# Empty instructions on TensorE from a fixed list, and the statistics' loads at other places, in a two-layer image block

## The chip, the core and the metric

The kernel runs on one core of a Trainium2 chip. The time is device microseconds of one execution. The engines are called PE (TensorE, the products; PEld is its loading of weights), DVE (VectorE), ACT (ScalarE), POOL (GpSimd) and SP (SyncE, which here only starts transfers).

## What is computed

Eight images of 384 channels and 64x64 pixels, in fp32, go through two layers, each with a residual. In the reference, with a group norm of 32 groups ahead of each layer:

```
# layer 0: layer norm over channels, qkv; the first 192 channels attend in 8x8 windows,
# the other 192 in windows shifted by 4 (4 heads of 48 each, bias by relative position)
x = x + proj(concat(win_attn(w1), win_attn(shifted w2, mask)))
# layer 1
t = einsum('bchw,oc->bohw', gn(x), w_in)            # 1x1 convolution
t = irfft2(rfft2(8x8 patches of t) * fft_filter)
t = depthwise_conv3x3(t, w_dw)
x = x + einsum('bchw,oc->bohw', gelu(t[:, :192]) * t[:, 192:], w_out)
```

## The kernel before

An image is cut into 8 strips of 8 rows (512 tokens, 3 channel tiles of 128 partitions). A *unit* is one strip of one of the two attention branches, so an image has 16 units; even units begin a strip. Everything of unit u is written as pieces with a place on a line, `at(place, piece, ...)` (L299), for example the three `qk_tile` pieces of a unit at 0.14, 0.34 and 0.55 of the unit before (L454; 3 channel tiles of weights, so 3 products of 512 columns each, written to pq), then `v_tile` (pvv), `scores` (pS, 64 small products), `exponent` and `divide` on DVE and ACT (tile e), `turn` (pT, transposes of e), `apply` (pA, 64 small products) and `put`; `project` (pr) is the output projection with its residual, three pieces a strip. Layer 1 of image b lies two units behind its own layer 0 and so beside layer 0 of image b+1: `mix` (pt, the 1x1 convolution), `transform` (pf, the 8x8 patches forward, then a product with feff on DVE), `back` (pz, inverse), `conv` (the 9 taps of the depthwise filter on DVE, tile zz, L758), `gate`, and `finish` (pw, the output product and residual x_finish). The plan is sorted by place at the end (L908), and that order is the program order of PE. All products are fp32 and take two passes, so a `matmul` gives four PE instructions (two weight loads, two products), a transpose two.

The helper `matmul` (L60) issues one product and then up to `share` empty instructions (`nop`, hint "empty") from the number that its piece has been given. The number comes from the end of the function (L908 to L926): at each marker `small_tiles` (L331, which itself does nothing) it takes the count of PE instructions so far, estimated from the table `FETCHES` and a guess of the waits, and finds n, the empties that bring the marker's run of small tiles to a given place modulo 256 (`RUN_AT`). If n is under 132, it spreads n over the `qk_tile` and `project` pieces since the last `scores`; otherwise it gives none. A marker stands ahead of two kinds of run: at the end of even units for images 1 to 7 (ahead of `ln_sums`, `transform`, `apply`, `transform`, `scores`: ln 32, pf 32, pA 128, pf 32, pS 128, 352 PE instructions, a *mixed run*), and at the end of odd units (ahead of `back`: pz 192, pA 128, pS 128).

Loads go through SP's queue; a load that is marked so waits for the first qk tile of its unit (`in_dense_work`, L325). A strip's *statistics* (L344: BNStats on DVE, tile st, fed by x_stats, 768 KB) feed the group norm of the first layer. For image b over 0 they are taken during image b-1, one strip per odd place and half a unit apart from its load (L806 to L812); `input_mean` and `input_std` follow in unit 10. The other loads of 768 KB a strip are x_norm, x_add, x_mix and x_finish, and out is stored.

Of the kernel before, what the change touches and what calls it, by code (L numbers as in the profile page):

```python
# [25 lines left out]
C_ID, C_ONES, C_GRP, C_FWD, C_INV, C_MASK = 0, 128, 256, 384, 512, 640  # L26
C_PICK = C_MASK + 3 * 64
N_CONST = C_PICK + 2
WAITS = 6.42, -38
FETCHES = {"qk_tile": 12, "v_tile": 24, "project": 12, "scores": 128, "apply": 128, "turn": 16,  # L30
           "ln_sums": 32, "mix": 12, "transform": 32, "back": 192, "finish": 48, "input_mean": 4,
           "input_std": 4, "second_mean": 4, "second_std": 4, "filter_weights": 4, "out_bias": 36,
           "qk_weights": 48, "spread_first": 16, "v_weights": 60}
RUN_AT = 208, 138


@with_exitstack
def block_kernel(ctx: ExitStack, tc: tile.TileContext, out, x, consts, fsel, wqk, wv, bqk, bv,
# [16 lines left out]

    fetched = {"count": 0, "empty": 0, "share": 0}

    def matmul(*args, **kw):  # L60
        tc.keep_in_program_order(nc.tensor.matmul(*args, **kw))  # L61
        fetched["count"] += 4

        n = min(fetched["empty"], fetched["share"])
        for _ in range(n):
            tc.keep_in_program_order(nc.tensor.nop(hint="empty"))
        fetched["empty"] -= n
        fetched["count"] += n

    def transpose(*args, **kw):  # L70
        tc.keep_in_program_order(nc.tensor.transpose(*args, **kw))  # L71
        fetched["count"] += 2

    def strip(tag, bufs, name):
        return sb.tile([P, KC, ST], F32, tag=tag, bufs=bufs, name=name)
# [85 lines left out]
    def filter_weights():  # L161
        pf = psum("pf")
        matmul(pf[:, 0:C], fsel_sb, filt_sb, start=True, stop=True)
        for h in range(2):
            nc.vector.tensor_copy(feff[h * 64:(h + 1) * 64], pf[h * 64:(h + 1) * 64, h * 192:(h + 1) * 192])
# [45 lines left out]
    def centre(w, *key):  # L211
        for k in range(KC):
            nc.scalar.activation(w[:, k], w[:, k], AF.Copy, scale=lng_sb[:, k:k + 1])
        pc = psum("pc")
        for k in range(KC):
            matmul(pc[:, 0:C], ones_c, w[:, k], start=(k == 0), stop=(k == KC - 1))
        means[key] = w, pc
# [5 lines left out]
    def qk_weights(br):  # L223
        pb = all_biases()[:, 3 * br:3 * br + 3]
        for j in range(3):
            for k in range(KC):
                matmul(pb[:, j:j + 1], wqk_sb[:, k, 3 * br + j, :], lnb_sb[:, k:k + 1],
                       start=(k == 0), stop=(k == KC - 1))
        centre(wqk_sb[:, :, 3 * br:3 * br + 3].rearrange("p k j c -> p k (j c)"), "qk", br)
# [71 lines left out]
    def at(place, piece, *args):  # L301
        plan.append((place, len(plan), piece, args))
# [64 lines left out]
    def summed(b, s):  # L367

        return b > 0 or s > 2
# [179 lines left out]
    def turn(b, s, br):  # L549

        nm = f"{b}_{s}_{br}"
        e = qks.pop((b, s, br, "e"))
        pT = psum2(f"pT_{nm}")
        for i in range(NS):
            transpose(pT[:, i // 4, i % 4 * P:(i % 4 + 1) * P], e[:, 2 * i:2 * i + 2, :], ident)
        eT = sb.tile([P, 2, ST], F32, tag="eT", bufs=1, name=f"eT_{nm}")
        nc.scalar.copy(eT, pT)
        qks[b, s, br, "eT"] = eT
# [163 lines left out]
    on_pe = {(B - 1, s): {1: 5} for s in range(NS - 1)}  # L722
# [83 lines left out]
    for b in range(B):  # L806
        first = 2 * NS * b

        for s in range(NS):
            u = first - 14.84 + s if b else -10 + 0.1 * s  # L810
            at(u, load, b, s, "stats")
            at(u + (0.5 if b else 0.05), input_stats, b, s)  # L812
        if b == 0:
# [18 lines left out]
        for s in range(NS):  # L832
            u = first + 2 * s
# [46 lines left out]
        for s in range(NS):  # L880
            u = first + 2 + 2 * s
# [24 lines left out]


    order = [p[2:] for p in sorted(plan, key=lambda p: p[:2])]  # L908
    count, dense, empty = fetched["count"], [], [0] * len(order)
    for i, (piece, args) in enumerate(order):  # L910
        count += 4 * sum(on_pe[args].values()) if piece is conv_taps else FETCHES.get(piece.__name__, 0)
        if piece in (qk_tile, project):
            dense.append(i)
        elif piece is scores:
            dense = []
        elif piece is ln_sums and not summed(*args):
            count += 64
        elif piece is small_tiles:
            n = (RUN_AT[args[0] % 2] - count - round(WAITS[0] * args[0] + WAITS[1])) % 256
            if n < 132:  # L920
                count += n
                for j in range(n):
                    empty[dense[j % len(dense)]] += 1
    for (piece, args), n in zip(order, empty):
        fetched["empty"], fetched["share"] = n, (n + 2) // 3
        piece(*args)  # L926
    assert fetched["count"] == count

# [103 lines left out]
```

## Time and profile before

| what | value |
|---|---|
| times of three runs, us | 3568.28, 3572.18, 3581.91 |
| median, us | 3572.18 |
| span of the profiled execution, us | 3571.7 |
| instructions in it (all engines) | 93732 |
| mean DMA rate, GB/s | 120 |
| DVE, depthwise taps L758 (zz), x1483 | 1117.8 us busy |
| PE, qk products (pq), x2160 | 999.8 us busy |
| PE, mix products (pt), x1536 | 536.0 us busy |
| PE, projection products (pr), x1152 | 522.5 us busy |
| SP's x_stats loads, x56, 768 KB each | 7.6 us from issue to landing |
| DVE wait for x_stats, 10 times | 19.1 us |

The profiled execution gives no time of its own apart from its span; the span lies 0.5 us below the median, and is what a sum from rows is made against. The second part of the page shows the span in 40 slices: the clock that TensorE was granted is full in all but the first slice, and PE is busy at nine tenths or more from the second slice to the last but one. A product's time in the rows is modelled at its end, so the distance between the starts of two of them is the better figure: six pq products take 2.57 us.

A row "issue" in the chain of waits is time in which an engine waited for nothing that the profile shows. Empty instructions have no rows of their own in the groups; they are counted in the built program, as is the place of an instruction modulo 256.

### The profile page before, as it was taken

Reading aid. Unit: us, or ns where it says so; the run is one execution under the profiler, and the core shown is the slowest. Engines: PE = TensorE matmul, PEld = TensorE weight load, DVE = VectorE, ACT = ScalarE, POOL = GpSimd, SP = SyncE. Lnnn points to the kernel's source line nnn. Section 1 sums busy time; section 2 is a strip of 40 time slices with the busy share of each in tenths; the row PEclk is TensorE's granted clock in tenths of the full one; section 3 lists DMA queues with packets and bytes.
Section 4 is the critical chain, followed back from the end, with each engine's and each line's share of the span. In section 5 each row is a group of like instructions: output and inputs, shape, how many; then the busy total and the mean of one; then the engine's idle time right before and its main releaser. Section 6 shows DMA issues by size and latency. Waiting matters only on the chain.

```text
span 3571.7 us, 93732 instructions
## 1 busy us (share of the span) xinstructions
PE 3489.3 (98%) x36598; PEld 2209.2 (62%) x36598; DVE 3059.8 (86%) x4370; ACT 2475.3 (69%) x3983; POOL 953.0 (27%) x1616
## 2 busy tenths in 40 slices
PE   7999999999999999999999999999999999999998
PEld 5666666666666666666666666666666656666554
DVE  4766689889988899888998889988899888887988
ACT  4777677768777677776777767777777768776442
POOL 5333222223222232222232223222232223221000
PEclk8999999999999999999999999999999999999999
DMA  4333333234333334333333334333334233333431
GB/s 124 115 124 111 104 113 133 101 105 158 127 121 116 114 125 158 103 112 134 126 130 124 118 106 143 133 103 134 123 120 148 100 106 122 100 104 108 156 116 72
DMA packets 177254, 427.45 MB, mean 120 GB/s; under 512 B 26784, under 2 KB 29371, under 8 KB 176840
## 3 DMA queue, kind: packets, MB, share of 16 engines
q1 hardware_dynamic: 139984, 370.54, 29.6%
q0 software_dynamic: 36416, 50.65, 5.1%
q8 instruction: 318, 5.21, 0.6%
q14 instruction: 96, 0.79, 0.1%
q10 hardware_dynamic: 440, 0.27, 0.0%
HBM read 270.21 MB, written 100.79 MB: 104 GB/s over the span
## 4 chain that ended last, share of the span: by engine, by line
PE 88%; DVE 8%; ACT 2%; DMA 1%; issue 1%; SPq 0%; ACTq 0%; DVEq 0%
PE pq L61 26%; PE pr L61 14%; PE pvv L61 13%; PE pt L61 11%; PE pw L61 6%; DVE zz L758 4%; PE pA L61 4%; PE pz L61 3%; PE pS L61 3%; PE pT L71 3%; PE pf L61 2%; PE ln L61 1%; DVE t L679 0%; DMA x_stats<-in_x_dram 0%; DVE e L535 0%
## 5 line engine op out<-in xcount | busy, mean ns | idle before, releaser
L758 DVE SCALAR_TENSOR_TENSOR zz<-z,dw_sb,zz 128x512 f32<-128x512 f32 x1483 | 1117.8, 783 | 26.2 <-ACT z L716 14.9
L61 PE MATMUL pq<-y,wqk_sb 128*128 128x512 f32 x2160 | 999.8, 600 | 0.9 <-DVE y L436 0.8
L613 POOL DMA_DIRECT2D oT<-o x960 | 480.4, 508 | 981.3 <-ACT z L716 442.4
L61 PEld LDWEIGHTS pq<-y,wqk_sb 128*128 128x128 f32 x2160 | 400.7, 190 | 459.9 <-issue 416.1
L61 PE MATMUL pt<-wi_sb,xn 128*128 128x384 f32 x1536 | 536.0, 487 | 7.6 <-ACT kcd L468 4.8
L61 PE MATMUL pr<-oT,wp_sb 128*128 128x512 f32 x1152 | 522.5, 592 | 0.0
L61 PE MATMUL pvv<-wv_sb,y 128*128 128x192 f32 x2880 | 508.5, 326 | 0.0
L61 PEld LDWEIGHTS pvv<-wv_sb,y 128*128 128x128 f32 x2880 | 470.7, 190 | 47.7 <-issue 32.7
L61 PEld LDWEIGHTS pt<-wi_sb,xn 128*128 128x128 f32 x1536 | 289.4, 190 | 234.9 <-issue 76.7
L450 POOL COPY y<-y 128x384 f32<-128x384 f32 x112 | 83.4, 744 | 1136.6 <-PE pvv L61 665.1
L61 PEld LDWEIGHTS pr<-oT,wp_sb 128*128 128x128 f32 x1152 | 218.6, 190 | 268.6 <-issue 249.9
L468 ACT ACTIVATE kcd<-pq,bqk_sb 32x512 f32<-32x512 f32 x512 | 348.4, 680 | 9.0
L468 ACT ACTIVATE qab<-pq,bq_sb,cst 96x512 f32<-96x512 f32 (+1 forms) x256 | 197.6, 772 | 199.2 <-PE pq L61 196.6
L501 ACT COPY v<-pvv 128x384 f32<-128x384 f32 x256 | 121.6, 475 | 212.6 <-PE pvv L61 211.4
L468 ACT ACTIVATE kab<-pq,bqk_sb 96x512 f32<-96x512 f32 (+1 forms) x256 | 174.1, 680 | 96.9 <-PE pq L61 92.4
L468 ACT ACTIVATE qcd<-pq,bq_sb,cst 96x512 f32<-96x512 f32 (+1 forms) x256 | 197.5, 772 | 35.9 <-PE pq L61 29.1
L662 ACT COPY t<-pt 128x384 f32<-128x384 f32 x256 | 122.5, 479 | 128.9 <-PE pt L61 124.8
L528 DVE TENSOR_TENSOR e<-pS,bias 128x512 f32<-128x512 f32 (+2 forms) x200 | 108.1, 547 | 114.6 <-PE pS L61 114.4
L380 POOL TENSOR_TENSOR sq<-sq 128x512 f32<-128x512 f32 x122 | 200.9, 1647 | 5.8
L535 DVE TENSOR_TENSOR e<-e,mx 128x1024 f32<-128x1024 f32 x128 | 198.7, 1553 | 4.1
L61 PE MATMUL pw<-zz,wo_sb 128*128 128x512 f32 (+1 forms) x512 | 183.4, 501 | 0.0
L545 DVE TENSOR_REDUCE rc<-e 128x16 f32<-128x1024 f32 x128 | 155.0, 1211 | 29.6 <-ACT e L540 29.6
(151 smaller groups left out, 5185.7 us busy)
## 6 DMA issues: line engine op xcount, KB each, us to landing
x_add<-in_x_dram SPq DMA_DIRECT2D x64, 768.0 KB, 9.6
x1d<-x_add SPq DMA_DIRECT2D x64, 768.0 KB, 3.7
x_mix<-x1d SPq DMA_DIRECT2D x64, 768.0 KB, 5.4
x_finish<-x1d SPq DMA_DIRECT2D x64, 768.0 KB, 7.2
out_dram<-x_finish SPq DMA_DIRECT2D x64, 768.0 KB, 4.2
x_norm<-in_x_dram SPq DMA_DIRECT2D x61, 768.0 KB, 7.4
x_stats<-in_x_dram SPq DMA_DIRECT2D x56, 768.0 KB, 7.6
oT<-o POOLq DMA_DIRECT2D x192, 96.0 KB, 3.8
```

Of the source, the lines that this page charges most:

```text
L61: tc.keep_in_program_order(nc.tensor.matmul(*args, **kw))
L71: tc.keep_in_program_order(nc.tensor.transpose(*args, **kw))
L380: nc.gpsimd.tensor_tensor(sq[:, 0, :], sq[:, 0, :], sq[:, k, :], ALU.add)
L450: nc.gpsimd.tensor_copy(dst[:, :, :, :, 0:4], src[:, :, :, :, 4:8])
L468: return nc.scalar.activation(dst[to:to + n], pq[of:of + n], AF.Identity, bias=bias[of:of + n], scale=scale)
L501: nc.scalar.copy(v[:, 384 * g:384 * (g + 1)], pvv[:, 0:384])
L528: nc.vector.tensor_tensor(e5[:, odd, :, a:z, :], pS[:, odd, :, a:z, :], bias_t[br, kind, odd].unsqueeze(2).to_broadcast([P, 2, z - a, 64]) ...
L535: zs["soft"] = nc.vector.tensor_tensor(e, e, mx.unsqueeze(2).to_broadcast([P, 2 * NS, 64]), ALU.subtract)
L545: nc.vector.tensor_reduce(rc, e, AX.X, ALU.add)
L613: nc.gpsimd.dma_start(out=oT[to % P:to % P + z - a, to // P, rows], in_=o[row + a:row + z, h // 2, of:of + n])
L662: nc.scalar.copy(t1, pt[:, 0:C])
L758: i = nc.vector.scalar_tensor_tensor(acc.rearrange("p (r c) -> p r c", c=SW), z[:, dy:dy + 8, dx:dx + SW], dw_sb[:, m, TAPS[tap]:TAPS[tap] ...
```

## The change

Two things. First, the statistics of image b (over 0) go by a list of places instead of one a unit and two apart:

```diff
+STATS_AT = 2.16, 2.40, 4.16, 5.16, 6.16, 7.16, 8.16, 9.16
...
-            u = first - 14.84 + s if b else -10 + 0.1 * s
+            u = first - 16 + STATS_AT[s] if b else -10 + 0.1 * s
             at(u, load, b, s, "stats")
             at(u + (0.5 if b else 0.05), input_stats, b, s)
```

In the same coordinates the places before were 1.16, 2.16, up to 8.16. So units 1 and 3 of an image lose the load and its BNStats, unit 2 gets a second and unit 9 one that it did not have.

Second, the empty instructions. The table `FETCHES`, the guess `WAITS`, the places `RUN_AT` and the count that `matmul` and `transpose` kept go out; a tuple holds a number for each `small_tiles` in order, and it is given without the limit of 132:

```diff
+EMPTY = (131, 235, 156, 217, 52, 171, 11, 172, 11, 124, 11, 116, 11, 124, 11, 124, 11, 45, 43, 124, 52, 123, 11, 124,
+...
+         11, 45, 43, 124, 52, 123, 11, 124, 11, 124, 11, 124, 11, 168, 245, 214)
...
-    count, dense, empty = fetched["count"], [], [0] * len(order)
+    dense, empty, counts = [], [0] * len(order), list(EMPTY)
     for i, (piece, args) in enumerate(order):
-        count += 4 * sum(on_pe[args].values()) if piece is conv_taps else FETCHES.get(piece.__name__, 0)
         if piece in (qk_tile, project):
             dense.append(i)
         elif piece is scores:
             dense = []
-        elif piece is ln_sums and not summed(*args):
-            count += 64
         elif piece is small_tiles:
-            n = (RUN_AT[args[0] % 2] - count - round(WAITS[0] * args[0] + WAITS[1])) % 256
-            if n < 132:
-                count += n
-                for j in range(n):
-                    empty[dense[j % len(dense)]] += 1
+            for j in range(counts.pop(0)):
+                empty[dense[j % len(dense)]] += 1
```

The built program has 81,410 PE instructions before and 82,442 after: the empties go from 7411 to 8443, and no other PE instruction is added. The numbers per piece change. Some of them, in the built programs, empties a piece:

| place | before | after |
|---|---|---|
| qk tiles of most even units, images 2 to 7 | 16 | 41, 42 |
| qk tiles and projections of unit 0, images 2 to 7 | 0 | 5 |
| qk tiles and projections of odd units from 5 on | 14, 15 | 1, 2 |
| qk tiles of unit 1 | 30, 31 | 14, 15 |
| qk tiles of unit 3 | 41, 42 | 17, 18 |
| qk tiles ahead of image 0's strip 6, branch 1 | 22 | 43, 44 |
| qk tiles ahead of image 0's strip 7, branch 1 | 0 | 78, 79 |
| qk tiles ahead of image 1's strips 1, 2, 3, branch 1 | 30, 32, 32 | 73, 57, 57 |
| first three projection pieces after the last scores | 12 | 105, 106 |
| last three projection pieces | 0 | 23, 24 |

## The prediction

> **What bounds the kernel now.** I read the page first, then the chain of waits over a few stretches, then the timeline at the places the chain names. The page says that TensorE sets the end:
>
> ```profile
> PE 3489.3 (98%) x36598; PEld 2209.2 (62%) x36598; DVE 3059.8 (86%) x4370; ACT 2475.3 (69%) x3983; POOL 953.0 (27%) x1616
> ...
> q8 instruction: 318, 5.21, 0.6%
> ...
> PE 88%; DVE 8%; ACT 2%; DMA 1%; issue 1%; SPq 0%; ACTq 0%; DVEq 0%
> ```
>
> PE is busy for 98% and carries 88% of the chain, so what the change is worth lies in the other 2%, about 80 us, and in PE instructions that do no work. The second line says where some of it goes. 5.21 MB in 318 packets is 16,384 bytes each; the built program has 81,410 PE instructions, and 318 x 256 = 81,408. So each packet is a block of 256 PE instructions, and PE can't go past one that has not landed. The chain in the middle of image 2, around the start of a mixed run (a run of layer 1's and layer 0's small tiles):
>
> ```profile
> 1007.99 0.62 PE pS L61 x41
> 1008.61 0.45 issue
> 1009.06 0.57 PE pS L61 x23
> ```
>
> pS, 64 small products, stops after 41 of them for 0.45 us without a releaser ("issue"). The packet of the next block was under way from 1006.60 to 1007.48, and the stop lies at an instruction that is the same one modulo 256 everywhere in the program where such stops are found. Small tiles use up a block in little time, so there a block comes late; between large products it does not. The second place is pA, the long run at the ends of units 1 and 3 of an image (a unit is one strip of one branch, from pS to pS). Unit 3 of image 5's stretch:
>
> ```profile
> 2147.17 4.28 PE pq L61 x8
> ...
> 2151.46 4.13 PE pq L61 x8
> ...
> 2162.48 0.01 PE pz L61
> 2162.49 0.35 PE pA L61 x19
> 2162.84 0.53 issue
> ```
>
> The stop of 0.53 us is one block's. The first two lines show another cost: in other units six pq products take 2.57 us, here eight take 4.28 and 4.13, thus 0.52 us each and not 0.43. In this unit each qk tile carries 41 or 42 empty instructions. Empties run at one in 70.9 ns where they stand in a row in the trace; a product of two passes takes 858 ns; so beyond some 11 empties per product PE's sequencer is the limit, not the array.
>
> **The blocks at mixed runs (even units' ends).** In the built program boundaries fell at instructions 52 and 308 of the run's 352 (47 and 303 in later images), which is in the first pf or pA and again in the pS; afterwards there is one boundary, at 232, in all of these runs. From the durations of units 5, 7, 9, 11, 13, 15 and 0 the stops in pS sum to 8.3 us above the floor of 24.3 us. I take all of it as gone; the bound is 4 us if the single boundary at 232, in pA, is late half as often, and 9.3 with unit starts. One more such stop in pS of the last strip, "issue" of 0.74 us in the chain at 3286.06 with a total of 0.95 against its like, goes too. [...] The trace has 0.2 to 0.66 us at the crossings inside runs of small tiles, and I go by it[...].
>
> **Units 1 and 3.** Two edits meet here. The statistics' loads of the next image (768 KB each) leave both units, and empties before unit 3's end drop from 41 or 42 per qk tile to 18 or 17 (unit 1: from 30 to 14). The pA runs' boundaries are unmoved (237 and 493), so only lateness of packets can fall. Of 11 stops of 0.56 to 1.93 us in pA (15.4 us), all are in units 1 and 3. The mean busy share of the DMA engines is 0.78 in unit 1 and some 0.55 in unit 3 at the packet, 0.3 to 0.46 elsewhere. The trace has its own experiment: image 7 has no next image, hence no statistics' loads, and its unit 3 has no stop and takes 18.07 us; images 2 to 6 take 19.57, 19.83, 20.36, 19.23 and 19.85, in all 8.5 more. Empties: 41 per tile cost 1.1 us per unit against 17, but the next transposes wait for VectorE's e anyway, so about 0.8 is left where VectorE is 98% busy (images 2 to 7) and 1.0 in image 1. Sum: 8.5 + 6 x 0.8 = 13.3, and 1.0; less 2.3, since VectorE, at 98% in unit 3 and above that in unit 4, takes over part of it even as it loses 1.88 us of statistics there: 12 us. Bounds: 8 (VectorE binds) and 16. Unit 1's stops are worth little: image 7 still has 1.22 us there without statistics' loads, and its units 1 and 2 sum to 47.67 us, against 47.53 to 47.61 with them (image 3: 49.02), since ScalarE is busy without a break (a table load, xn, o) and pw waits for its o. I take 1.5 us.
>
> **Where the statistics go.** Unit 2 gets two loads and two times BNStats (1.88 us of VectorE a strip), unit 9 gets one. SP's queue issues one more 768 KB load in unit 2, past x_mix and x_add; the page has 7.6 us from issue to landing. Issued at about 1698.3 in image 4's stretch (with the first qk tile of unit 2), it lands at 1703.6 to 1706. VectorE takes its queue in order: behind the waiting BNStats stand e of the next unit and the taps of the depthwise filter, and PE's transposes wait for e. Before, VectorE waited for x_stats for 19.1 us in ten waits, mostly in image 0. In unit 1 VectorE waits 2.04 us for x_norm already, which then moves earlier. So the wait is between nothing and 2 us an image; I take 0, because at the end of unit 2 it has the whole unit to land. Unit 9 loses nothing: VectorE was idle for 2.62 us at the start of unit 10, and pm, the group mean's product, still comes 7.6 us into that unit.
>
> **The one-off runs.** The old rule left out a run that wanted 132 empties or more; the list does not. In the first and last images there are few pieces to spread them over, and none lies beside slack. Counts are those of the built program:
> - Ahead of pS of image 0's strip 6, branch 1 (44 per qk tile, before 22): +1.8 us.
> - Ahead of pS of strip 7, branch 1 of image 0: 235, so 79, 78, 78 on three qk tiles, before none. 235 x 0.0709 + 0.6 = 17.3 us; the three tiles took 3 x 2.57 = 7.7: about +9.2 us after the queue's lead. The unit took 15.3 us with PE 100% busy, nothing hides it.
> - Image 1, strip 1, branch 1: 217 (73 each, before 30), with the mix's products between: +2.5, part of it under PE's wait for xn up to 414.13 (1.35 us "issue" in the chain and ScalarE's 2.17 before).
> - Strips 2 and 3 of image 1: 57 per tile, before 32: +1.35 each, 2.7.
> - Even units in general: 41 per qk tile, before 16, but mix products stand between, and PE's queue is 2.2 to 2.9 us ahead after pw: hidden. If that cover were gone, 1.1 us in each of about 7 x 7 units, over 50 us; the smallest slack I find is 0.19 us, so I take 0.
> - The end: 245 and 214 after the last scores, on six projection pieces. The first three get 106, 106, 105 (before 12), i.e. 36 per product; the other three 24 more on each, hidden. 317 x 0.0709 + 0.9 = 23.4 us from 3314.8, so the transposes that started at 3324.0 go out at 3338.2, +14.3 us.
>
> The chain there:
>
> ```profile
> 3323.87 0.14 issue
> 3324.01 1.07 PE pT L71 x8
> 3325.07 1.95 PE pz L61 x94
> 3327.09 0.93 PE pA L61 x62
> 3328.02 4.15 PE pw L61 x24
> 3332.17 1.94 PE pt L61 x6
> 3334.11 5.15 PE pr L61 x12
> ```
>
> From 3324.0 to 3356 it is PE only, then VectorE takes over with work that waits for that PE work. I let the whole tail move by 14.3. Bounds: 7, if VectorE's backlog of taps is what binds (it is 95% busy from 3314 to 3357: 40.88 of 43 us), and 15.
>
> **The sum.** Gains: 8.3 + 0.95 + 12 + 1.5 = 22.8. Costs: 1.8 + 9.2 + 2.5 + 2.7 + 14.3 = 30.5. The net is +7.7 us on the span of 3571.7, which is 0.5 below the median of the three runs (3568.28 to 3581.91). Forecast: 3580 us. A measurement of this kernel can tell about 0.5% from no change, 17.9 us.
>
> **Rivals.** *The tail and image 0 absorb their empties.* For it: VectorE's 95% in the tail. Against: PE is the chain there. Then the costs are some 7 us: 3571.7 - 22.8 + 7 = 3556; with gains at their upper bounds 3550. If only the tail absorbs half, 3572. *VectorE waits for x_stats in unit 2* (the slower side): one mechanism, at the BNStats moved into unit 2, price 2 us in each of images 1 to 6's stretches, and it takes unit 3's 12 us away, because VectorE is 98% busy in unit 3 and can't make it up. 3571.7 - 10.8 + 30.5 = 3591. It decides from about 1.5 us of wait per image. Against it: the load has most of a unit. *The change doesn't do what it says*: boundaries sit where they should, but the crossing at 232 is in pA, where small products run as quickly, and blocks could be as late there. Then the 9 us are not gained: 3571.7 + 7.7 + 9.2 = 3589.
>
> **How the numbers follow.** Forecast with its own range 3567 to 3590: 0.56. Tail partly absorbed, around 3570: 0.12. First rival: 0.11. Second: 0.12. Third: 0.09. Over 0.5% faster (below 3554) is only the first rival's better part, 0.08; over 0.5% slower (above 3590) are most of the second rival (0.08), nearly half of the third (0.04) and the sixth of the forecast in which a cost at its bound or the even units' cover comes in (0.09): 0.21; between, 0.71. The range 3561 to 3597 leaves out the first rival's lower half and the second's upper end.
>
> **What would show it.** Right: no "issue" in pS of mixed runs; pq in unit 3 back at 0.43 us a product; units 3 near 18 us; the unit ahead of image 0's last pS at some 24.5 us and not 15.3; pT of the last strip at 14 us after its e is ready. Wrong: stops in pA at the new boundary, a VectorE wait for x_stats in unit 2, pq in even units above 2.6 us, or an end in which VectorE never waits for the late transposes.

## The result and the profile after

The changed kernel takes 3586.07 us (median of six runs, 3582.21 to 3590.72) against 3569.49 for the kernel before (median of six runs). The ratio is 1.0041 with a 95% interval of 1.0031 to 1.0052, so it is slower by some 15 us. Its profiled execution took 3582.21 us with a span of 3580.4, and in every other run listed the time is 1.8 us above the span too; that is the quickest of the six, while the profiled execution of before (span 3571.7, so some 3573.5 us) was 4 us slower than its median. So the two spans are only 8.7 us apart, and the medians 16.6. A second profile of the changed kernel (e8 below) has 3584.4, and its time, 3586.14, is close to the median.

The page of the profile after, first its busy times, then the instruction blocks, then the chain's shares by engine:

```profile
PE 3484.3 (97%) x36598; PEld 2203.9 (62%) x36598; DVE 3069.5 (86%) x4370; ACT 2477.6 (69%) x3983; POOL 949.0 (27%) x1616
...
q8 instruction: 322, 5.28, 0.6%
...
PE 84%; DVE 12%; ACT 2%; issue 1%; DMA 1%; SPq 0%; POOL 0%; ACTq 0%; DVEq 0%
```

There are four more blocks (322 for 318), which is the 1032 empties. PE's share of the chain fell from 88% to 84%, and VectorE's rose from 8% to 12%: part of what PE no longer waits for, VectorE now sets. The chain of waits at the mixed run of image 2 shown in the prediction now reads:

```profile
1014.86 0.65 PE pf L61 x16
1015.52 0.93 PE pS L61 x64
1016.45 2.77 PE pq L61 x6
```

All 64 products of pS run in 0.93 us and nothing stands between them. From start to start of pS, units 5, 7, 9, 11, 13 and 15, each of which begins with the pS of a mixed run, take 24.26 us in every image from 1 to 7. (Unit 0, which the prediction names with them, follows the other kind of run; it takes 43.70 us in images 2 to 7, before and after.)

The boundary at 232 is the ninth instruction of pS, since ln, pf, pA and pf ahead of it are 224; it is not in pA, as the prediction has it. The packed traces show what did change. In 40 of these runs in images 1 to 7 of the kernel before, the block from 52 to 308 holds small products alone; its 256 instructions are gone 2.5 us after PE entered it, or up to 3.3 us with a stop. The packet of the next block starts 0.1 to 1.0 us after that entry and takes 0.9 to 1.5, and PE goes on 1.2 to 1.6 us after the packet's end. In the last unit's run the packet starts 0.5 us ahead of that entry and has ended 2.1 us before PE goes on. In the changed kernel the block that ends at 232 begins among large products and lasts 5.03 us, and its successor's packet has ended 5.4 to 6.5 us before PE needs it. pS of these units adds up to 46.1 us before and 36.3 after.

Ahead of image 0's last pS the chain is this (the pair of lines is one product of two passes, and the empties behind it; cut):

```profile
327.65 1.10 PE pq L61 x2
328.75 0.91 issue
...
```

Nine such products make 17 us where the three tiles took 7.7. The end looks the same, on the projections:

```profile
3316.48 2.04 PE pr L61 x2
3318.52 0.60 issue
...
3332.33 1.93 PE pT L68 x8
```

A product and its 36 empties take 2.6 us here, and the transposes of the last strip begin 25.2 us after the last pS (3307.1), where it was 10.1 before. The place where the forecast's largest error lies is VectorE in units 2 and 3, image 5:

```profile
2136.12 0.60 DVE st L257
...
2138.90 1.29 DVE st L257 x2
...
2140.83 0.60 DVE st L257
...
2142.36 0.60 DVE st L257
...
2143.62 0.60 DVE st L257
...
2148.86 1.27 DVE e L524 x3
...
2156.32 1.24 DVE e L543
2157.55 0.14 issue
2157.69 1.06 PE pT L68 x8
```

The chain is VectorE's from 2121 to 2158. Six BNStats, two strips' worth, stand shortly ahead of unit 3's softmax (e), and the transposes wait for it. In this profile unit 3 has no stop in pA any more (e8 still has one in images 3 and 5), but it takes 18.7 to 19.4 us in images 2 to 6, and 16.53 in images 1 and 7.

### The profile page after: what moved, and what is told of

The parts are those of the page before. It is cut to its first block, busy times and chain, and to the rows that moved or that the text cites. A ratio compares the mean times of both kernels' runs of the same rounds, so it can differ in the third digit from the quotient of the medians.

```text
span 3580.4 us, 94755 instructions
## 1 busy us (share of the span) xinstructions
PE 3484.3 (97%) x36598; PEld 2203.9 (62%) x36598; DVE 3069.5 (86%) x4370; ACT 2477.6 (69%) x3983; POOL 949.0 (27%) x1616
## 4 chain that ended last, share of the span: by engine, by line
PE 84%; DVE 12%; ACT 2%; issue 1%; DMA 1%; SPq 0%; POOL 0%; ACTq 0%; DVEq 0%
PE pq L61 25%; PE pr L61 14%; PE pvv L61 13%; PE pt L61 10%; PE pw L61 6%; DVE zz L754 6%; PE pA L61 3%; PE pz L61 3%; PE pT L68 3%; PE pS L61 3%; PE pf L61 2%; PE ln L61 1%; DVE e L531 1%; DVE t L675 1%; DVE st L257 1%
## 5 line engine op out<-in xcount | busy, mean ns | idle before, releaser
L61 PE MATMUL pr<-oT,wp_sb 128*128 128x512 f32 x1152 | 530.0, 598 | 7.8 <-issue 7.3
L619 DVE SCALAR_TENSOR_TENSOR x_add<-pr,vec,x_add 128x512 f32<-128x512 f32 x192 | 142.9, 744 | 49.9 <-PE pr L61 49.2
```

The source lines that it names most:

```text
L619: after_softmax(nc.vector.scalar_tensor_tensor(t[:, m, :], pr, bp_sb[:, m:m + 1], t[:, m, :], ALU.add, ALU.add))
```

## The experiments

Each kernel was timed beside the kernel before on the same chip, and the ratio is to that. Between experiments ratios are compared, not times, since the medians of before lay between 3569.5 and 3575.8 us. A unit's time is from the start of its pS to that of the next, taken from each run's one profile. The first pS starts 63.3 to 68.1 us into the twelve profiles, and none of these edits reaches it.

**e1: no empties after the last scores.**

```diff
-         11, 45, 43, 124, 52, 123, 11, 124, 11, 124, 11, 124, 11, 168, 245, 214)
+         11, 45, 43, 124, 52, 123, 11, 124, 11, 124, 11, 124, 11, 168, 0, 0)
```

> The changed kernel with the last two numbers of the list (245 and 214, the empties after the last scores) set to 0; all else as changed. Theory: the end lost 15.5 us because 317 empties at 70.9 ns stand ahead of the last strip's transposes, so this gives 3571 us against 3586 (ratio to the kernel before 1.0003), and from the last pS to the end 258 us against 273.3. Rival, the tail's loss comes from something else (VectorE's taps, transfers): no change, 3586, 273 us.

Measured: 3570.4 us, ratio 0.9986 (0.9979 to 0.9993). From the last pS to the end it is 255.6 us, against 273.3 (changed) and 257.8 (before, which had 105 empties there, 36 of them on the first three projections; the list's last two numbers are 459, with 315 on these three and the rest on six more behind). The chain of this kernel there:

```profile
3317.04 1.24 DVE e L543
3318.28 0.14 issue
3318.41 1.06 PE pT L68 x8
```

The transposes wait for e again, as before the change, 10.1 us after the last pS. The end's loss is the empties', and the tail does move as a whole; the rival is out.

**e2: the large one-off numbers of images 0 and 1 cut as well.**

```diff
-EMPTY = (131, 235, 156, 217, 52, 171, 11, 172, 11, 124, 11, ...
+EMPTY = (0, 0, 10, 89, 52, 43, 11, 44, 139, 124, 11, ...
```

> As the run without the end's empties, and also the large one-off numbers of images 0 and 1 cut (131, 235, 156, 217, 52, 171, 11, 172, 11 become 0, 0, 10, 89, 52, 43, 11, 44, 139; all later runs keep their places modulo 256; some runs of images 0 and 1 lose theirs). Theory: images 0 and 1 get back 11.3 us (two units of image 0) and 5.7 (three of image 1), less about 1 of block stops where a run has lost its place: 3555 us, ratio 0.996. Rival, placing those runs was worth what it cost: as the first run, 3571.

Measured: 3551.94 us, ratio 0.9931 (0.9917 to 0.9945). The two units of image 0 are back at 15.30 us (17.09 and 24.80 in the changed kernel), the three of image 1 at 24.34, 25.20 and 24.38 (28.83, 25.99, 26.05). From the first pS to the last it is 14.3 us less than in the changed kernel. Several of the first runs have lost their places, and of the units of images 0 and 1 only the second of these three shows a loss against before (25.20 for 24.38). Placing these runs was not worth its price.

**e3: the changed empties, the statistics at their old places.**

```diff
-            u = first - 16 + STATS_AT[s] if b else -10 + 0.1 * s
+            u = first - 14.84 + s if b else -10 + 0.1 * s
```

> The changed kernel with the statistics at their places of before (the empties as changed). Theory: moving them was worth 5.6 us in image 0 (units 0, 1 and 4 there) and some 4 over units 3 and 4 of images 1 to 7, with stops in pA at the end of units 1 and 3 back: 3596 us, unit 3 of images 2 to 6 at 19.5 us, image 7's at 16.5. Rival, in units 3 and 4 the move only swapped a block stop for a VectorE limit: 3591, with image 0's loss alone.

Measured: 3587.12 us, ratio 1.0033 (1.0020 to 1.0046): no difference from the changed kernel that can be told. Image 0 is longer (units 0 to 14 sum to 286.8 us, against 280.3 and 282.0 in the two profiles of the changed kernel), but here the first pS came 2.1 and 3.5 us earlier than in those. From the last pS of image 1 to that of image 7 it is 2560.2 us against 2559.8 and 2560.4. Unit 3 of images 2 to 6 takes 19.0 to 19.3 us, with the stops in pA back and e ready 0.9 to 1.6 us earlier in the unit. In image 5:

```profile
2161.45 1.07 PE pT L68 x8
...
2166.48 0.35 PE pA L61 x19
2166.83 1.00 issue
```

The rival was right for images 1 to 7: the move swapped a block's stop for a longer wait on VectorE.

**e4: the empties of before, only the statistics moved.**

```diff
-            u = first - 14.84 + s if b else -10 + 0.1 * s
+            u = first - 16 + (2.16, 2.40, 4.16, 5.16, 6.16, 7.16, 8.16, 9.16)[s] if b else -10 + 0.1 * s
```

> The kernel before with only the statistics moved. Theory: it keeps the 8 us of stops in pS of the mixed runs, pays none of the one-off costs, gains 5.6 us in image 0 and a few in units 3 and 4: 3560 us, ratio 0.997. If the DMA-late blocks were all of unit 3's excess and the 41 empties per tile were free, units 3 are at 18.1 as in image 7 and the time is 3555; if VectorE's statistics in unit 2 bind, units 3 stay at 18.7 to 19 and it is 3562.

Measured: 3567.62 us, ratio 0.9977 (0.9969 to 0.9985), last pS 5.0 us earlier than before. That gain is image 0's: its units 0 to 14 sum to 269.0 us against 274.6. Of these 5.6, 3.9 are units 2 and 4; the other 1.7 are unit 0's, and e8 shows below that they are not the edit's. From the last pS of image 1 to that of image 7 it is 2576.7, 1.6 more than before; unit 3 of images 2 to 6 takes 18.3 to 19.2, and units 3 and 4 of images 2 to 7 gain 1.8 us in all. There are no stops in pA of unit 3 any more, but the chain is that of PE with its empties (in images 2, 3 and 6 the first of its qk products also wait for VectorE's tile t). In image 5 all of the unit's qk products are:

```profile
2140.43 4.17 PE pq L61 x8
2144.61 5.17 PE pq L61 x10
```

That is 9.3 us, where e7 below takes 7.92. The forecast of 3560 counted more in units 3 and 4 than is there.

**e5: 32 mixed runs with their block boundaries at 52 and 308 again.**

```diff
-..., 124, 11, 116, 11, 124, 11, 124, 11, ...
+..., 48, 87, 40, 87, 48, 87, 48, 87, ...
```

> The changed kernel, but in 32 mixed runs of images 1 to 7 (ahead of units 5, 7, 9, 11, 13, 15 where the list has 124 or 116 followed by 11) 76 empties stand behind the run and not ahead of it, so the block boundaries fall at instructions 52 and 308 of the run, as before, and not at 232. All other runs keep their places. Theory: the stops in pS come back, 0.27 us a run as before: +8 us against the changed kernel in this call, units 5 to 15 at 24.3 to 24.9 us and not at 24.26. Rival, [...] something else took the stops away: no change and 24.26.

Measured: 3594.54 us, ratio 1.0056 (1.0044 to 1.0069), against 3586.14 for the changed kernel on the same chip (e8): +8.4. The 32 runs are those of units 7 to 15 (9 to 15 in image 1, 7 to 11 in image 7); those of unit 5 stayed, though the expectation names it. Units that begin with a moved run take 24.3 to 25.0 us, the others 24.26. pS of units 5 to 15 adds up to 44.9 us against 36.3 in e8, so the loss is inside pS and not in the empties that now stand behind it. A stop in the chain of this kernel, at a run of image 7:

```profile
2892.74 0.62 PE pS L61 x41
2893.36 0.44 issue
2893.80 0.57 PE pS L61 x23
```

It is the picture of before, after 41 products, by nothing but 76 empties that stand behind the run and not ahead of it: the block before this stop is again one of small products alone. The even units, which now have 16 empties a tile for 41, stay at 28.25 us: there 41 cost nothing.

**e6: no placing at all.**

```diff
-EMPTY = (131, 235, 156, 217, 52, 171, 11, 172, 11, 124, 11, ...
+EMPTY = (0, 0, 0, 0, 0, 0, 0, 0, 0, 0, 0, ...
```

> The changed kernel with all numbers of the list at 0: no empties for placing, runs stand where they fall. Theory: images 0 and 1 and the end give back about 33 us, and of 112 runs about half get one stop of 0.3 to 1 us, about 30 us in all, minus what VectorE hides: 3575 us, near the kernel before. Rival, [...]: 3552, as the run with the one-off numbers cut.

Measured: 3577.79 us, ratio 1.0008 (1.0002 to 1.0015). Without a single empty the kernel is 0.3% quicker than the changed one and no quicker than before. Against e2 it is 0.8% longer by the two ratios, some 27 us, and that is what placing is worth after its own cost. In its chain, at a run of the other kind (pz, pA, pS):

```profile
2112.72 2.08 issue
2114.80 0.98 PE pS L60 x51
```

At another it is 1.11 us. Both are longer than any stop in pS before the change (0.74, at 3286.06).

**e7: e2 with the statistics out of unit 2, the group mean a unit later.**

```diff
-STATS_AT = 2.16, 2.40, 4.16, 5.16, 6.16, 7.16, 8.16, 9.16
+STATS_AT = 4.16, 5.16, 6.16, 6.66, 7.16, 8.16, 9.16, 10.16
...
-        at(first - 5.8 if b else -8, input_mean, b)
-        at(first - 5.4 if b else -7.9, input_std, b)
+        at(first - 4.8 if b else -8, input_mean, b)
+        at(first - 4.4 if b else -7.9, input_std, b)
```

In the list, the 116 and 11 of each image are 124 and 3 here (and 10 is 7), so that the runs keep their places.

> The run with the one-off numbers and the end cut, with the statistics also out of unit 2: places 4.16, 5.16, 6.16, 6.66, 7.16, 8.16, 9.16, 10.16, the group mean one unit later (with the counts set so that the runs keep their places). Theory: in images 2 to 6 VectorE has 3.8 us less to do in unit 2 ahead of unit 3's e, so unit 3 goes from 18.7 to 16.5 us as in image 7: up to 10 us, less 2 that unit 4 gives back: 3544 us, ratio 0.991. Rival, VectorE is short over units 1 to 11 as a whole: the time only moves to later units, 3552.

Measured: 3538.86 us, ratio 0.9904 (0.9890 to 0.9917), the quickest of all. Unit 3 of image 5 in its chain:

```profile
2119.84 0.93 PE pS L61 x64
2120.77 7.92 PE pq L61 x18
2128.70 1.95 PE pvv L61 x12
2130.65 0.87 PE pT L68 x8
```

PE is the chain throughout: 18 passes, two for each of nine products, in 7.92 us (0.44 each), then the transposes without a wait. Unit 3 is 16.53 us in all of images 1 to 7.

**e8: the changed kernel again.** 

> The changed kernel once more, on the chip of this call, to compare with: 3586 us, ratio 1.004.

Measured: 3586.14 us, ratio 1.0038 (1.0025 to 1.0050).

**e9 and e10: the two edits of e7 apart.** Both stand on e2. e9 has e7's group mean and list with the changed kernel's `STATS_AT`; e10 has the mean in its old place, e2's list, and `STATS_AT = 4.16, 5.16, 6.16, 6.66, 7.16, 8.16, 8.66, 9.16` (the last two earlier than in e7, since the mean is).

> The run with the one-off numbers and the end cut, and of the late statistics' edits only the group mean one unit later (unit 11 for 10); the statistics stay as in the changed kernel. Theory: of the 14 us that both edits gave, unit 10 had 1.5 us in each of images 1 to 6, where VectorE ran the group mean's small steps between the softmax's; so unit 10 goes from 29.7 to 28.25, unit 11 gives 0.45 back, unit 3 stays at 18.7: 3545 us, ratio 0.9915. Rival, the late strips alone did all: 3552 and 29.7.

> As the run before, but the group mean stays in unit 10, and only the statistics leave unit 2 (places 4.16, 5.16, 6.16, 6.66, 7.16, 8.16, 8.66, 9.16). Theory: unit 3 at 16.54 us in images 2 to 6 for 18.7, unit 4 at 29.0 for 28.6, unit 10 stays at 29.7: 3544 us, ratio 0.991. Rival, VectorE is short there anyway: unit 3 stays at 18.7 and the time at 3552.

Measured: e9 3543.15 us, ratio 0.9924 (0.9909 to 0.9938); e10 3547.95, ratio 0.9928 (0.9913 to 0.9944). Both shifted their unit as expected: in e9 unit 10 takes 28.25 us for 29.7 and unit 11 0.45 more; in e10 unit 3 takes 16.53. From the first pS to the last, e2 takes 3227.5 us, e9 3222.2, e10 3227.4 and e7 3213.8. So in the profiles e9 keeps 5.3 of the 7 us forecast and e10 none of its 8, while both edits together gain 13.7. In e10 units 7 and 9 grow by 0.3 us an image each and units 1 and 4 by 0.4 each, as e7's rival had it. In e9 unit 2 takes 32.0 us in four images, for 30.0, and unit 3 there 0.9 less. Why unit 2 takes 30 in some executions and images and 32 in others stays open. By the times, it is not shown that e9 and e10 beat e2, whose interval overlaps theirs (and each was profiled in its slowest execution); e7 beats it narrowly (the two intervals touch at 0.9917).

## Why the prediction was right, and where its terms were off

The sign, the size within the range and the two costs that carry it were right. That the sum came so close is partly luck, since a gain that was left out makes up for more than half of one that was booked too high. The terms against the first profile of the changed kernel (units 2, 4 and 6 of image 1 stand in a row of their own, and are left out of the rows above it):

| step | forecast, us | measured, us | by |
|---|---|---|---|
| mixed runs, stops in pS | -8.3 | -10.1 | units 5 to 15; e5 |
| last strip's unit 14 | -0.95 | -1.0 | units |
| units 3 and 4, images 1 to 7 | -12 | -5.3 | units; e3, e4, e10 |
| units 1 and 2 | -1.5 | -1.6 (e8: -0.9) | units |
| image 0, two units ahead of pS | +11.0 | +11.3 | units; e2 |
| image 1, three units | +5.2 | +5.8 | units; e2 |
| after the last scores | +14.3 | +15.5 | last pS to end; e1 |
| image 0, statistics | none | -3.9 | units; e3, e4 |

The measured column sums to +10.6 us for +7.7. The span grew by 8.7; the other -1.9 are unit 0 of image 0 and the time ahead of the first pS, which e8 does not have. Against e8 the span grew by 12.7, and 4 us more lie between before's one profile and its median.

The empties' cost was a plain sum, and it held: a count from the built program by 70.9 ns, less what the products cover. For the even units the cover was there, as the forecast had it (28.25 us with 41 empties a tile and with 16).

For the mixed runs the price held: -8.3 came from a floor rounded to 24.3 us, and over 41 units at 24.26 it is -10.1. The place did not hold: the boundary at 232 lies in pS like the one at 308. What took the stops away is the longer time between one boundary and the next (5.03 us for 2.5), as told with the result. The prediction's premise, that PE can't go past a block that has not landed, agrees with the traces of before and after: where two products of pS or pA start over 0.25 us apart (31 times before, 6 after), it is at the same place modulo 256, to one instruction; the second starts 1.2 to 1.6 us after the end of the packet ahead of it, and no block anywhere is entered sooner than 1.19 us after its packet. So the packet's end alone is not the limit; the prediction's own example ended at 1007.48 and PE went on at 1009.06. Where a block lasts over 10 us, among large products, the next packet has ended 8.3 us or more before PE needs it.

The term that failed is that of units 3 and 4. The step was to take image 7's unit 3, without statistics, as what the others would become. Two things were wrong in it. First, image 7's VectorE has no BNStats in unit 2 either, while in the changed kernel unit 2 has two strips of them, late and just ahead of unit 3's e. I had put "between nothing and 2 us" on a wait for the transfer there and took 0. The transfer was in time (VectorE goes into the BNStats without a wait in images 2 to 6), but the work itself is 1.9 us a strip on an engine that is full, and images 2 to 6 take 2.1 to 2.9 us more in unit 3 than image 7. Image 1 has the same statistics and takes 16.53 too: there VectorE is busy for 49% of unit 2, for 92 to 95% in images 2 to 6. e10 takes the statistics alone out of unit 2, and the excess is gone. Second, the gain that did come is not the statistics' alone. With the new empties and the old statistics (e3) unit 3 is already 4.9 us shorter over images 2 to 7, with the moved statistics and the old empties (e4) 3.7, and with both 5.1 and 6.1 in two profiles. The stop in pA, the empties on the qk tiles and VectorE's e are three limits of this unit. e3 still has the first and the third, e4 has the second, and the changed kernel has the third. That the transposes of unit 3 waited for e anyway, as the prediction says, does not hold for before: in images 3, 5 and 7 its chain there is PE's own, under 41 empties a tile. In image 7, which has no statistics to move, empties of 17 for 41 gave 1.5 us; the forecast had 0.8 to 1.0.

A gain was left out altogether: image 0. There the loads of the next image's statistics were on the chain of before:

```profile
123.23 9.68 DMA x_stats<-in_x_dram
132.91 0.02 issue
132.94 1.88 DVE st L261 x3
```

The BNStats that stand at the start of unit 4 wait for a transfer of 9.68 us, with the softmax queued behind them: pS ended at 133.0, and its first e starts at 136.5, behind the BNStats and three steps more. The waits of before listed 19.1 us for x_stats, mostly in image 0; I read that line and priced nothing for it. With the statistics moved, unit 4 runs through on PE:

```profile
130.55 7.92 PE pq L61 x18
138.47 1.95 PE pvv L61 x12
```

Units 4 and 2 are back at 15.30 us, for 18.64 and 15.85. The sum of the waits would have been no guide: it is 22.4 us in the changed kernel, but none of them stands ahead of unit 4's softmax. Another 1.7 us of the first profile in image 0's unit 0 isn't the change's: twelve passes of pq take 5.35 us there and 7.04 in e2, and e8, which is the same kernel, has the longer unit.

So -5.3 for -12 is 6.7 us too much gain booked, -3.9 for 0 takes back more than half of that, and the other rows agree within 1.8 us each. Of the rivals, the absorbed tail is refuted by e1. Late blocks at the new boundary are refuted for the mixed runs by the units at 24.26 us and by e5, which has the boundaries back at 52 and 308 and the stops with them. The slower one, VectorE held by statistics in unit 2, is what happened in kind, but by the statistics' work and not by a wait for the transfer, and at some half of its price. Nor did e5 and e6 equal their counterparts, as their rivals had it: e5 lost 8.4 us to the changed kernel, e6 some 27 to e2.

## What to carry over

Filler ahead of a critical place is free only where something covers it: count the instructions per product, multiply by the measured cost of one, and compare with the product's own time; where a product takes 858 ns, 36 fillers at 71 ns are 2.6 us, while 41 a tile beside the mix products of the even units cost nothing (28.25 us with 41 and with 16). When one of two limits on a stage is removed, look up what the other would give before the gain is booked, and look at where the moved work lands in the order of the engine that is already full. In the mixed runs a block was late where its predecessor was used up in 2.5 us and not where that took 5.03, with the boundary in pS both times, so what to look for there is how long PE takes from one boundary to the next, not which tile the boundary is in. And a list made for the middle of a loop should be checked at its ends, where the pieces that cover it are missing: nearly all the loss of this change was there, and without it the kernel is faster than before by 0.7%.

## What was not expected of the hardware

In the traces of before and after, no packet of a block starts more than 302 instructions before PE enters that block. In the mixed runs of before a block's 256 instructions of small products were gone in 2.5 us, and from the start of the next block's packet to PE going on it was 2.3 to 2.9 us: a packet and the wait behind it took about as long as the block. The stops that are longest do not come from long packets. The longest of before stands in pA (1.72 us at 1252.49), and its packet took 0.98 us, where those ahead of the stops in pS took 0.9 to 1.5; but it starts 3.7 us after PE entered the block ahead. At all stops in pA, before and after, this is 1.7 to 3.7 us, with packets of 0.9 to 1.1; why they start later there is not shown. And a run without stops is repeatable: units 5, 7, up to 15 take 24.25 to 24.26 us in every image from 1 to 7 of the changed kernel's first profile, so a placement of these runs can be judged from one profile, though the times of whole runs of the changed kernel spread over 8 us.
